# A graph-attention kernel: another head turned by VectorE in the first tile of each batch element, one head's copies moved to VectorE, and four small transposes moved between two others

## The chip, the cores and the metric

The kernel runs on one core of one Trainium2 chip. The metric is device time in microseconds (us) of one execution. Three executions of the kernel before took 3004.06, 3004.3 and 3010.76 us; their median is 3004.3 us.

## What is computed

The input is x with 16 batch elements of 1024 nodes and 256 features, and an integer adjacency matrix of 1024 x 1024 for each batch element. Two layers follow each other:

```python
# layer 0: masked attention, 8 heads of 32 features
h = relu(layernorm(x))
Q, K, V = h @ Wq.T + bq, h @ Wk.T + bk, h @ Wv.T + bv        # per head
scores = Q @ K.T * 32 ** -0.5;  scores[adj == 0] = -inf
x = x + (softmax(scores) @ V) @ Wo.T + bo
# layer 1: scores of the nodes with themselves, weighted by a vector for each kind of edge
h = relu(layernorm(x))
e_k = leaky_relu((h * a_k) @ h.T, 0.2)                       # symmetric
scores = e_k where adj == k + 1, else -9e15
x = x + softmax(scores) @ h
```

All data is fp32 (adj is int32). The inputs hold only the values 0 and 1 in adj, so layer 1 needs the first kind of edge alone; a second program for more kinds stands behind a branch and isn't run.

## The kernel before

**Tiles and steps.** A batch element is cut into 8 tiles of 128 rows (t = 0 to 7). The main loop has one step for each of the 128 tiles and one more. A step holds the work of several tiles at once, written out by hand in a loop over the heads h = 0 to 7: layer 0's attention of the present tile (`now`), the end of layer 0 of the tile before (`was`), layer 1 of a tile 9 steps back (`edge`) and 10 steps back (`edge_was`), and the projections of a tile 9 steps ahead (`piece`). The order on each engine is the order of this program; nothing reorders it. A step takes some 22 to 23 us, and mostly 25 to 27 us for t = 0.

**One head of layer 0.** TensorE makes the scores (L461, two matmuls into one half of PSUM's score space). VectorE adds the mask and takes the row's extreme in one instruction (L473, `softmax_max`). ScalarE takes the exponential (L490, `softmax_exp`, one turn of the loop later). Then the 128 x 1024 matrix must be turned, since the product with V needs the keys on the partitions. There are two ways:

- `turn`: 8 transposes of 128 x 128 on TensorE into two PSUM buffers of 128 x 512 (L590), each copied to SBUF into `pT` (L591). The copy is VectorE's for heads 0, 1, 4 and 5 (`MIXED`), ScalarE's for 2, 3, 6 and 7, unless the caller names an engine.
- `turn_blocks` and `place_blocks`: one VectorE instruction turns all blocks of 32 x 32 (L381), and 4 DMAs of 128 KB on SP's queue put the blocks where they belong in `pT` (L386).

`by_blocks(t)` tells which heads go the second way: 0, 1, 4 and 5 in tiles 1 to 6; 0, 1 and 4 in tile 7; 4 and 5 in tile 0. Heads in `MIXED` have their keys in another order, which suits the blocks. Where such a head is turned by TensorE after all, ScalarE's exponential writes with a permuted pattern into another buffer.

**Order around the change.** In turn h of a step: `scores(h)`; `softmax_max(h)`; `softmax_exp(h-1)`; head h-2 is turned. With t = 0, heads 5 and 6 of the tile before (`was`) are turned in turn h = 0, one after the other, head 5 with ScalarE's copies. Then `edge.score(0)` follows: the left half of layer 1's scores, for which a tile with t > 0 takes blocks that were kept from earlier tiles and transposes them (L627). In step t = 0 the edge tile has t = 7, so `score(0)` is 4 transposes. In turn h = 4 of a step with t = 0, `block` runs: it is `edge_was.gather(0)` (L698, 32 matmuls that read layer 1's turned matrix, placed by 4 DMAs that were issued in turn 0), then `was.combine(1)` (L526, 64 matmuls). The turn of head 2 is put off to turn h = 5 (`late_turn`), where heads 2 and 3 are turned one after the other, both with ScalarE's copies.

**SP's queue** issues, in program order: the keys of the next batch element (L360, 8 loads of 512 KB, spread over step t = 7 and the next step t = 0 by `KEY_STEPS`; the loads for heads 4 to 7 stand in turns 0, 2, 3 and 4 of step t = 0), the queries of the next tile (L428, turn 3), the block placements (L386), the stores of layer 0's result (L552) and of the output (L708). Each issue waits for the landing of the one 8 before it, because the queue's DMAs share 8 semaphores in turn. POOL's queue carries the other DMAs.

The lines that the text names: L461 scores, L473 softmax_max, L490 softmax_exp, L590/L591 turn_half, L381 blocks_of, L386 placed, L360 load_key, L428 load_queries, L526 combine, L698 gather, L627/L633 score, L656 edge.softmax_max, L541 output, L547 residual, L182/L183 layer norm statistics, L237/L249/L250 turn of the piece, L355 biased, L536 combined.

Of the kernel before, what the change touches and what calls it, by code (L numbers as in the profile page):

```python
# [24 lines left out]
NEG_INF = -9000000000000000.0  # L25
MASKED = -1e30
MIXED = (0, 1, 4, 5)
BY_BLOCKS = {7: (0, 1, 4), 0: (4, 5)}


def by_blocks(t):
    return BY_BLOCKS.get(t, MIXED)

# [14 lines left out]
def gnn_kernel(  # L48
# [18 lines left out]
    nc = tc.nc  # L67
# [719 lines left out]
    with tc.manual_schedule():  # L787
# [42 lines left out]
        piece, edge, edge_was = piece_next, None, None  # L830
# [8 lines left out]
        for s in range(B * NT + 1):  # L839
            b, t = divmod(s, NT)  # L840
# [7 lines left out]
            late_turn = None  # L848
# [14 lines left out]
            for h in range(HEADS):  # L863
# [49 lines left out]
                if h == 4 and not late_scores:  # L913
                    block()
                    late_turn = turning
                    load_keys(h, 1)
                    continue
                if h == 5 and late_turn:
                    late_turn.turn(2, 0)
                    late_turn.turn(2, 1)  # L920
                if h == 0 and t == 0 and was:
                    for half in range(2):
                        was.turn(HEADS - 3, half, nc.scalar.copy)
                if turning and th in by_blocks(turning.t):
                    turning.turn_blocks(th)
                    turning.place_blocks(th)
                elif turning and (h, t) != (HEADS - 1, NT - 1):
                    turning.turn(th, 0)
                    turning.turn(th, 1)
# [3 lines left out]


                if h == 0:
                    if edge:
                        edge.score(0)
                    if gone:
                        gone.normed()
                    if edge_was:  # L940
                        edge_was.turn_blocks()
                        edge_was.place_blocks()
# [57 lines left out]
            gone, was, now, nxt = was, now, nxt, nxt2  # L1000
            edge_was, edge = edge, edge_nxt
# [8 lines left out]
        for i in range(1, len(tiles) + 2):  # L1010
            edge = tiles[i] if i < len(tiles) else None
# [75 lines left out]
```

## Time and profile before

| | |
|---|---|
| runs | 3004.06, 3004.3, 3010.76 us |
| the profiled execution's own time | 3006.89 us |
| its span (first to last instruction) | 3005.0 us |
| TensorE clock granted | 0.998 |
| busy: TensorE, ScalarE, VectorE, GpSimd | 2903.3, 2635.5, 2495.4, 2171.0 us |
| DMA moved | 704.03 MB, mean 234 GB/s |

The profile is one execution. The page counts the busy time of each engine, groups the instructions by line and tile, and names for idle time what ended it. The timeline lists the instructions of a window in order of time; the windows view gives each engine's busy time and the share of time in which the 16 DMA engines were busy; the issue view gives the time from a DMA's issue to its landing. Times within a step are given below as us from the start of the span.

### The profile page before, as it was taken

To read this page: it belongs to the slowest core of one execution; us is meant where nothing else is said; L and a number is where in the kernel's file an instruction comes from. 1 tells how busy PE (TensorE), PEld (TensorE's weight loads), DVE (VectorE), ACT (ScalarE), POOL (GpSimd) and SP (SyncE) were. 2 spreads that over 40 slices of the span, in tenths; PEclk is the share of its full clock that TensorE was granted. 3 is DMA by queue.
4 is the path that set the end of the run, shared out by engine and by line. 5 is a ranking of instruction groups with operands and counts; after the bars stand their busy time and mean duration, and the time that the engine had idled before them with its cause. 6 is when DMAs were issued, how large, how long until landed. Compare 5 with 4: busy or idle time off the path is not lost. (4 is left out here: it accounts for less than half of the span.)

```text
span 3005.0 us, 95721 instructions
## 1 busy us (share of the span) xinstructions
PE 2903.3 (97%) x36594; PEld 2234.0 (74%) x36594; DVE 2495.4 (83%) x4405; ACT 2635.5 (88%) x5191; POOL 2171.0 (72%) x2999
## 2 busy tenths in 40 slices
PE   7889999999999999999999999999999999999998
PEld 5777777777777777777777777777777777777664
DVE  5888888888888888878888887888888888788875
ACT  5999989999898999999999998998989999898882
POOL 3767877777787777778778777777877777786542
PEclk9999999999999999999999999999999999999999
DMA  7787877778778887877878777787787878777763
GB/s 243 233 259 215 248 229 243 250 227 261 227 227 254 239 260 218 243 247 230 269 222 245 239 237 249 227 267 222 231 255 232 263 219 243 245 230 250 196 174 100
DMA packets 607041, 704.03 MB, mean 234 GB/s; under 512 B 64305, under 2 KB 537777, under 8 KB 606577
## 3 DMA queue, kind: packets, MB, share of 16 engines
q1 hardware_dynamic: 537504, 485.68, 54.4%
q0 software_dynamic: 66960, 210.04, 21.7%
q8 instruction: 294, 4.82, 0.7%
q10 hardware_dynamic: 2112, 2.10, 0.2%
q14 instruction: 171, 1.39, 0.1%
HBM read 252.98 MB, written 134.22 MB: 129 GB/s over the span
## 5 line engine op out<-in xcount | busy, mean ns | idle before, releaser
L473 DVE CUSTOM_DVE_ANT_0 p<-s,neg 128x1024 f32<-128x1024 f32 x1024 | 1238.6, 1210 | 344.8 <-PE s L461 324.6
L490 ACT ACTIVATE p<-p,nmx 128x1024 f32<-128x1024 f32 x1024 | 1236.4, 1214 | 51.6 <-DVE nmx L473 43.1
L461 PE MATMUL s<-k,qt 128*128 128x512 f32 x2048 | 743.2, 445 | 30.4 <-DMA k<-kd 8.3
L591 ACT COPY pT<-trp 128x512 f32<-128x512 f32 x1056 | 566.5, 593 | 77.5 <-PE trp L590 77.1
L590 PE MATMUL trp<-ident,p 128*128 128x128 f32 x4480 | 587.3, 274 | 27.4 <-ACT pT L591 15.0
L590 PEld LDWEIGHTS trp<-ident,p 128*128 128x128 f32 x4480 | 516.0, 140 | 118.9 <-ACT pT L591 30.2
L381 DVE STREAM_TRANSPOSE blocks<-p 128x1024 f32<-128x1024 f32 x472 | 585.2, 1240 | 11.1 <-ACT p L680 10.6
L526 PE MATMUL acc<-pT,v 128*32 128x128 f32 x16384 | 507.8, 273 | 9.3 <-ACT full L309 8.9
L526 PEld LDWEIGHTS acc<-pT,v 128*32 128x32 f32 x16384 | 453.4, 110 | 80.9 <-issue 36.1
L698 PE MATMUL acc<-h,pT 128*32 128x256 f32 x8192 | 510.0, 381 | 1.9 <-DMA pT<-blocks 1.6
L441 POOL TENSOR_SCALAR neg<-adj 128x1024 bf16<-128x1024 int32 x128 | 467.8, 3655 | 11.9 <-ACT neg L453 1.9
L676 POOL TENSOR_TENSOR sel<-sel,less 128x1024 f32<-128x1024 f32 x120 | 287.8, 2398 | 201.7 <-ACT less L665 201.7
L461 PEld LDWEIGHTS s<-k,qt 128*128 128x128 f32 x2048 | 312.4, 190 | 153.0 <-issue 82.5
L698 PEld LDWEIGHTS acc<-h,pT 128*32 128x32 f32 x8192 | 265.3, 110 | 190.7 <-issue 48.8
L633 PE MATMUL s<-h1T,ha 128*128 128x512 f32 (+2 forms) x744 | 272.8, 490 | 2.8 <-ACT h1T L569 2.8
L490 ACT ACTIVATION_READ_ACCUMULATOR p<-p,nmx 128x1 f32 x1024 | 213.3, 208 | 0.0
L330 POOL DMA_DIRECT2D kd<-halves x240 | 172.1, 766 | 35.5 <-POOL halves L314 35.4
L314 POOL TENSOR_TENSOR halves<-full,halves 128x256 fp32r<-128x256 f32 x240 | 176.5, 735 | 20.0
L674 POOL TENSOR_SCALAR less<-top 128x1 f32<-128x1 f32 x120 | 31.9, 266 | 213.0 <-DVE top L656 212.9
L647 ACT COPY mirror<-s 128x128 f32<-128x128 f32 (+3 forms) x208 | 76.1, 393 | 122.5 <-DVE top L656 102.9
L324 POOL DMA_DIRECT2D qd<-halves x240 | 177.8, 787 | 7.1
L633 PEld LDWEIGHTS s<-h1T,ha 128*128 128x128 f32 x744 | 126.7, 190 | 70.8 <-issue 44.8
(117 smaller groups left out, 4321.3 us busy)
## 6 DMA issues: line engine op xcount, KB each, us to landing
pT<-blocks SPq DMA_DIRECT2D x2368, 128.0 KB, 3.6
qt<-qd SPq DMA_DIRECT2D x128, 512.0 KB, 4.7
k<-kd SPq DMA_DIRECT2D x128, 512.0 KB, 6.8
adj<-in_adj POOLq DMA_DIRECT2D x127, 512.0 KB, 6.1
qd<-halves POOLq DMA_DIRECT2D x240, 256.0 KB, 4.0
kd<-halves POOLq DMA_DIRECT2D x240, 128.0 KB, 4.3
xb<-in_x POOLq DMA_DIRECT2D x128, 128.0 KB, 4.9
x1d<-x SPq DMA_DIRECT2D x128, 128.0 KB, 5.1
```

The costliest lines, as they stand in the source:

```text
L324: nc.gpsimd.dma_start(out=qds[self.b][self.first, oc].rearrange("p u w n -> p u (w n)"), in_=halves.unsqueeze(1).to_broadcast([P, 2, 2 * P]),)
L381: nc.vector.transpose(blocks.rearrange("p b j q -> p j b q"), p)
L441: nc.gpsimd.tensor_scalar(self.neg, self.adj, 0.0, MASKED, ALU.is_equal, ALU.mult)
L461: nc.tensor.matmul(self.ps[:, cols], lhsT=self.qt[:, h, :], rhs=keysets[self.b][h][:, cols], start=True, stop=True,)
L473: nc.vector.tensor_tensor_reduce(out=p, in0=sides[h in self.second], in1=self.neg, scale=-SCALE, scalar=FLOOR, op0=ALU.add, op1=ALU.min, a ...
L490: nc.scalar.activation(to, of, AF.Exp, bias=nmx, scale=-1.0, accum_out=self.sums[:, h : h + 1])
L526: nc.tensor.matmul(sums_place[r * HD : (r + 1) * HD, g * P : (g + 1) * P], lhsT=vs[self.b][:, j, place_of(h) : place_of(h) + HD], rhs=self ...
L590: nc.tensor.transpose(tr[:, j, :], p[:, jj * P : (jj + 1) * P], ident)
L591: copy(pT[:, half * 4 : half * 4 + 4, :], tr)
L633: nc.tensor.matmul(self.side[:, cols], lhsT=self.ha[:, c, :], rhs=h1T[:, c, cols], start=(c == 0), stop=(c == NC - 1),)
L676: nc.gpsimd.tensor_tensor(self.sel, self.sel, self.less, ALU.subtract)
L698: nc.tensor.matmul(self.sums[a * HD : (a + 1) * HD, :], lhsT=self.pT[:, j, a], rhs=h1s[self.b][:, j, :], start=(j == 0), stop=(j == NT - 1),)
```

## The change

Three edits, all in steps with t = 0 (one for each of the 16 batch elements, and the last step for the third edit):

1. Head 0 of tile 0 goes by blocks: VectorE's block transpose and 4 DMAs take the place of 8 TensorE transposes and 2 VectorE copies. Its exponential is then written in plain order, in place.
2. The two copies of head 2, turned late, go to VectorE instead of ScalarE.
3. `edge.score(0)` stands between the turns of heads 5 and 6 of the tile before instead of after both.

```diff
-BY_BLOCKS = {7: (0, 1, 4), 0: (4, 5)}
+BY_BLOCKS = {7: (0, 1, 4), 0: (0, 4, 5)}
...
                 if h == 5 and late_turn:
-                    late_turn.turn(2, 0)
-                    late_turn.turn(2, 1)
+                    late_turn.turn(2, 0, nc.vector.tensor_copy)
+                    late_turn.turn(2, 1, nc.vector.tensor_copy)
                 if h == 0 and t == 0 and was:
                     for half in range(2):
                         was.turn(HEADS - 3, half, nc.scalar.copy)
+                    if edge:
+                        edge.score(0)
...
                 if h == 0:
-                    if edge:
+                    if edge and (t or not was):
                         edge.score(0)
```

## The prediction

> **What bounds the kernel now.** I read the page's busy times first, then the timeline of one step with t = 0, then the DMAs of that step.
>
> ```profile
> PE 2903.3 (97%) x36594; PEld 2234.0 (74%) x36594; DVE 2495.4 (83%) x4405; ACT 2635.5 (88%) x5191; POOL 2171.0 (72%) x2999
> ```
>
> TensorE is busy 97% of the span, so eight transposes less should count in full: 16 steps of about 1 us. But that is an average. The change touches steps with t = 0 alone, so one of these must be read; I took the one from 1288.26 to 1313.97 us. TensorE's timeline there (start, duration, instruction, idle time before it):
>
> ```profile
> 1288.83 1.04 PE L590 MATMUL trp<-ident,p 128*128 128x128 f32 x8
> 1290.11 1.15 PE L590 MATMUL trp<-ident,p 128*128 128x128 f32 x8 [0.24 <-ACT pT L591]
> 1291.09 0.60 PE L627 MATMUL s<-ident,mirror 128*128 128x128 f32 x4
> 1291.44 0.72 PE L461 MATMUL s<-k,qt 128*128 128x512 f32 x2
> ...
> 1293.90 0.71 PE L461 MATMUL s<-k,qt 128*128 128x512 f32 x2
> 1294.92 1.15 PE L590 MATMUL trp<-ident,p 128*128 128x128 f32 x8 [0.30 <-ACT pT L591]
> 1295.90 0.49 PE L627 MATMUL s<-ident,mirror 128*128 128x128 f32 x3
> ...
> 1299.69 2.57 PE L698 MATMUL acc<-h,pT 128*32 128x256 f32 x31
> ...
> 1304.15 0.73 PE L461 MATMUL s<-k,qt 128*128 128x512 f32 x2
> ...
> 1306.11 1.04 PE L590 MATMUL trp<-ident,p 128*128 128x128 f32 x8
> 1307.46 1.14 PE L590 MATMUL trp<-ident,p 128*128 128x128 f32 x8 [0.32 <-ACT pT L591]
> 1308.36 0.71 PE L461 MATMUL s<-k,qt 128*128 128x512 f32 x2
> ```
>
> The three bracketed waits are what the edits aim at: 5/6 (edit 3), head 0 (edit 1), 2/3 (edit 2). The line between them matters more: the gather L698 takes 2.57 us here. Later in the same step 32 matmuls of L698 stand at 1.93 us (1310.36). It waits inside, for its matrix `pT`, which SP's DMAs place. SP's timeline and, for the fourth of these placements (issued 1294.64), the issue view:
>
> ```profile
> 1291.62 0.55 SPq L360 DMA_DIRECT2D k<-kd  x1
> 1292.28 3.96 SPq L386 DMA_DIRECT2D pT<-blocks  x4
> 1296.28 1.30 SPq L360 DMA_DIRECT2D k<-kd  x2
> ...
> ```
>
> ```profile
> DMA to landing us min/median/max: 5.9/5.9/5.9
> ```
>
> So the last of the four pieces lands at 1300.52, 12.26 us into the step, and the scores of head 5 start at 1304.15, which is 3.63 us later: just 32 matmuls of L698 (pitch 1.75, from 1310.36 to 1312.11) and 64 of L526 (1.86, from 1312.11 to 1313.97). I took the same two times in the other steps with t = 0. In batch elements 4, 9 and 14 the fourth piece lands 13.87, 11.56 and 13.41 us into the step, head 5's scores start at 17.50, 15.20 and 17.04, and the steps take 27.31, 25.00 and 26.86 us. The first difference is 3.63 to 3.64 in all 14 steps that have a gather, and 9.8 us follow it in 13 of them. The steps differ only in when that DMA lands. The windows view says why it is late:
>
> ```profile
> 1288.26:1304.15 15.89, 15.35 (x180) 13.00 (x177) 11.05 (x19) 14.75 (x27) 10.10 (x18) 1.00 1.03 373
> ```
>
> The last two columns: the DMA engines are busy all the time (1.03) at 373 GB/s. Four loads of keys and one of queries, 512 KB each, crowd here. **In a step with t = 0 the DMA queue, not TensorE, sets when the second half starts.**
>
> **The change part by part.** *Edit 1* removes 8 transposes and their wait: from the scores at 1293.90 to L627 at 1295.90 are 2.00 us, and scores alone have a pitch of 0.56 (1308.36 to 1308.91 shows 0.55), so TensorE gains 1.44 us. VectorE gives up two copies (1.28 as a pair at 1295.80) for one block transpose (1.24, L381): level. ScalarE writes head 0's exponential in order: 2.16 us at 1292.28 against 1.16 for an unpermuted one, 1.0 us less. SP gets 4 issues of 128 KB. *Edit 3*: head 6's transposes wait for the PSUM buffer that ScalarE copies until about 1290.05; the four of L627 (pitch 0.35) now fill this time, and head 6 starts no later than now, so TensorE gains 0.35.
>
> Both lie before the gather, 1.79 us together, and neither moves its matrix: that comes from VectorE's transpose of `sel`, which needs only the step's first scores, and its DMAs stand on SP behind the key loads, ahead of the new issues. TensorE would reach head 3's scores at 1295.9, before their keys land: that load was issued at 1289.86 and landed at 1296.56. Head 4's keys land at 1298.64, and the gather's last piece at 1300.52. So the gain turns into waits at L461 and L698. **I cost edits 1 and 3 at nothing.** Cover gone, they are worth up to 1.79 us a step; 1.2 if head 4's scores wait for VectorE's L656, which head 0's block transpose and L656 itself (1.24 + 1.19) put at about 1297.8 against scores at 1299.05 now.
>
> The new DMAs: their first can go out when VectorE's transpose ends: head 2's `softmax_max` starts 0.35 earlier than now and ends at 1295.5, 1.24 more make 1296.7. Each issue then waits for the landing of the eighth before it. They go out from 1296.7 to 1299.3, and the loads of head 6's and 7's keys follow instead of going out at 1296.94 and 1298.66. 512 KB at 369 GB/s (the DMA rate of this stretch) are 1.42 us of DMA time; SP's four issues are 2.4 to 2.6 us. Head 7's keys, which landed at 1306.34 (7.68 after the issue), would land between 1307.8 and 1308.9; they are read at 1309.72. That is covered, and so are head 6's, which land earlier and are read at 1308.36. The queries loaded between them are for the next step.
>
> *Edit 2* lies behind the gather, where nothing hides it. ScalarE's pair of copies takes 1.08 us and starts 0.71 after the transposes (1306.82 against 1306.11). VectorE is free at 1306.23, so its pair starts as soon as the first half is there, 0.64 after (what an idle ScalarE shows elsewhere: transposes at 1404.52, copy at 1405.16), and takes 1.28. Its second copy ends 1.92 after the transposes' start instead of 1.79; the second half of head 3's transposes waits for it. **That is 0.13 us a step lost.** Bounds: a gain of 0.32 if the whole wait went, a loss of 0.35 if all of the pair's 0.20 and another 0.15 of a late start counted. I take 0.13, since the rows are direct. On VectorE the copies push residual and norms (1306.37 to 1308.00) behind 1308.03, and head 6's `softmax_max` from 1309.11 to about 1309.7. Next in line would be the next step's first scores, which need head 7's: these end at 1312.61 and the scores start at 1313.97, so 1.36 us cover 0.6. ScalarE's 1.08 us less release nobody: its next copies wait for TensorE (0.26 idle at 1308.16).
>
> *Other steps.* In the first step of all (41.1 to 67.7) there is no gather; ScalarE is late there and head 3's transposes wait 0.96 us, while VectorE is free: 0.8 us gained. In the step at 198.8 (no gather either) head 7's `softmax_max` ends only 0.22 us before the next scores: the copies cost about 0.4.
>
> Sum: 14 x 0.13 - 0.8 + 0.4 = +1.4 us on the profiled execution's 3006.89 us (span 3005.0), so 3008.3. That execution is 2.6 us above the median of 3004.3; on the median I forecast 3005.7, say 3006.
>
> *The skill on two points.* The Trainium skill, "DMA: Bandwidth & Descriptors", section "Queues, rings and completion order", says that an engine takes a ring's descriptors in order but that completion isn't first in, first out. In this trace the pieces land before the keys that were issued after them (1300.52 against 1301.81), so the rows speak for order; by the page's warning the sum would be that of the second rival below. "VectorE: DVE Perf Modes", section "Rules for kernel authors", would leave a full 128 x 128 turn to TensorE. By that rule edit 1 is to be left out, and the sum would lose its part, which the rows put at nothing anyway.
>
> **The rivals.** *The gate gives way.* If the placements landed earlier, or the waits inside L698 were small, the gains would reach the step's end: 1.2 to 1.79 us in 14 steps, less 1.4 above, 15 to 24 us: 2980 to 2989 (I take 2986). For it speaks the 97%; against it the constant 3.63 us in 14 of 14 steps.
>
> *The new DMAs push the gate.* They go out from 1296.7 on, while the gather's pieces are still under way (until 1300.52). If the 16 DMA engines shared their time among all that is under way, these pieces would land up to 1.42 us later; past zero it decides at once, since the gather has no slack. Price: 14 x 1.42 + 1.4 = 21 us: 3026. Against it: the next keys, 512 KB, went out at 1296.28 already, and still landed after.
>
> *Edit 2 gains instead.* The 2/3 wait of 0.32 goes: 14 x 0.32 + 0.8 = 5 us less: 2999, still within the bound. That the change does something else than it says I exclude: the program's instruction order holds the three moves as told and no others.
>
> **How the numbers follow.** Forecast 0.70; edit 2 gains 0.12; the gate gives way 0.10; the DMAs push it 0.08. About 0.3% (9 us) is what a measurement of this kernel can tell from no change. Faster 0.10, same 0.82, slower 0.08. The range takes in the forecast, edit 2's bounds (14 x -0.32 and +0.35: 2999 to 3009), the runs' own spread (6.7 us above the median) and a part of both outer rivals: 2992 to 3016.
>
> **What would show it.** Right: in steps with t = 0 the start of head 5's scores still follows the fourth placement's landing by 3.63 us and that landing stays 11.6 to 13.9 us into the step; TensorE's waits move from L590 to L461 and L698, named DMA; head 3's transposes still wait about 0.3 us, now for VectorE. Wrong: steps with t = 0 shorter by over a microsecond, the landing at another time, or waits for keys at heads 6 and 7.

## The result, and the profile after

| | kernel before | changed kernel |
|---|---|---|
| median of 20 runs (lowest, highest), us | 3010.15 (3003.87 to 3012.76) | 3014.53 (3006.91 to 3019.45) |
| the profiled execution's own time; span, us | 3006.89; 3005.0 | 3012.56; 3010.7 |

The ratio is 1.0017 [1.0009, 1.0024]: some 5 us slower, which by the prediction's bound of 0.3% is "the same". The forecast of 3006 is 8.5 us too low. Of that, 5.9 us are the base: the three runs shown had a median of 3004.3, and 20 runs have one of 3010.15. The rest is the change: the medians differ by 4.4 us, and the forecast gave it 1.7 (1.4 before rounding).

The busy times on the changed kernel's page:

```profile
PE 2888.7 (96%) x36466; PEld 2218.8 (74%) x36466; DVE 2517.8 (84%) x4421; ACT 2602.5 (86%) x5159; POOL 2167.4 (72%) x2999
```

TensorE is busy for 14.6 us less than before (2903.3), and the span is longer. To see why, read a step with t = 0 again. This is TensorE's timeline of the changed kernel in the same batch element as in the prediction; the step begins at 1291.91:

```profile
1292.48 1.03 PE L590 MATMUL trp<-ident,p 128*128 128x128 f32 x8
1293.35 0.60 PE L627 MATMUL s<-ident,mirror 128*128 128x128 f32 x4
1293.79 1.11 PE L590 MATMUL trp<-ident,p 128*128 128x128 f32 x8
1294.65 0.71 PE L461 MATMUL s<-k,qt 128*128 128x512 f32 x2
1297.16 0.71 PE L461 MATMUL s<-k,qt 128*128 128x512 f32 x2
1297.70 0.49 PE L627 MATMUL s<-ident,mirror 128*128 128x128 f32 x3
...
1301.48 0.70 PE L461 MATMUL s<-k,qt 128*128 128x512 f32 x2 [1.73 <-DVE top L656]
1303.49 0.69 PE L461 MATMUL s<-k,qt 128*128 128x512 f32 x2 [0.43 <-DMA k<-kd]
1304.17 2.59 PE L698 MATMUL acc<-h,pT 128*32 128x256 f32 x31
...
1308.65 0.73 PE L461 MATMUL s<-k,qt 128*128 128x512 f32 x2
...
1311.99 1.25 PE L590 MATMUL trp<-ident,p 128*128 128x128 f32 x8 [0.35 <-DVE pT L591]
```

L627 now stands between the two turns, and their wait of 0.24 us is gone; head 0's transposes and their 0.30 us are gone too. The time comes back as waits of 1.73 and 0.43 us at the scores of heads 3 and 4. (The 1.73 is put down to VectorE's L656, but that stands behind head 3's scores in the program and can't have held them; head 3's keys landed at 1301.35, just before the scores.) The late turn still waits, 0.35 us, now for VectorE. SP's timeline of the same step shows the four new issues at 1301.42, ahead of the keys of heads 6 and 7:

```profile
1295.42 3.84 SPq L386 DMA_DIRECT2D pT<-blocks  x4
1299.30 0.84 SPq L360 DMA_DIRECT2D k<-kd  x1
1301.42 3.17 SPq L386 DMA_DIRECT2D pT<-blocks  x4
1304.64 0.62 SPq L360 DMA_DIRECT2D k<-kd  x1
1305.37 0.54 SPq L428 DMA_DIRECT2D qt<-qd  x1
1305.95 0.59 SPq L360 DMA_DIRECT2D k<-kd  x1
```

The gather's fourth piece was issued at 1297.96, and its issue view answers:

```profile
DMA to landing us min/median/max: 7.1/7.1/7.1
```

It lands at 1305.02, and head 5's scores start 3.63 us later, as before.

I took the same times in all steps with t = 0 of batch elements 2 to 15, in each kernel. "Landing" is that of the fourth piece; "rest" runs from head 5's scores to the step's end. All are means in us, the two landings and head 7's scores from the step's begin:

| kernel | length | landing | head 5's scores after it | rest | head 7's keys land | head 7's scores |
|---|---|---|---|---|---|---|
| before | 25.93 | 12.58 | 3.63 | 9.71 | 18.24 | 21.69 |
| changed | 26.46 | 12.80 | 3.69 | 9.96 | 21.19 | 22.20 |

### The profile page after: what moved, and what is told of

Its sections match the earlier page's. It is cut to its first block, busy times and chain, and to the rows that moved or that the text cites. A ratio compares the mean times of both kernels' runs of the same rounds, so it can differ in the third digit from the quotient of the medians.

```text
span 3010.7 us, 95592 instructions
## 1 busy us (share of the span) xinstructions
PE 2888.7 (96%) x36466; PEld 2218.8 (74%) x36466; DVE 2517.8 (84%) x4421; ACT 2602.5 (86%) x5159; POOL 2167.4 (72%) x2999
## 3 DMA queue, kind: packets, MB, share of 16 engines
q0 software_dynamic: 66960, 210.04, 21.6%
## 5 line engine op out<-in xcount | busy, mean ns | idle before, releaser
L490 ACT ACTIVATE p<-p,nmx 128x1024 f32<-128x1024 f32 x1024 | 1218.3, 1196 | 53.3 <-DVE nmx L473 51.1
L461 PE MATMUL s<-k,qt 128*128 128x512 f32 x2048 | 743.7, 445 | 56.0 <-DMA k<-kd 28.4
L591 ACT COPY pT<-trp 128x512 f32<-128x512 f32 x1024 | 549.9, 592 | 99.9 <-PE trp L590 99.6
L381 DVE STREAM_TRANSPOSE blocks<-p 128x1024 f32<-128x1024 f32 x488 | 605.0, 1240 | 12.3 <-ACT p L680 10.6
L590 PE MATMUL trp<-ident,p 128*128 128x128 f32 x4352 | 571.5, 274 | 20.4 <-ACT p L490 13.0
L590 PEld LDWEIGHTS trp<-ident,p 128*128 128x128 f32 x4352 | 502.6, 141 | 105.0 <-ACT p L490 26.5
L698 PE MATMUL acc<-h,pT 128*32 128x256 f32 x8192 | 508.4, 381 | 2.1 <-DMA pT<-blocks 2.0
L461 PEld LDWEIGHTS s<-k,qt 128*128 128x128 f32 x2048 | 312.0, 190 | 182.7 <-issue 91.1
L698 PEld LDWEIGHTS acc<-h,pT 128*32 128x32 f32 x8192 | 263.3, 110 | 191.9 <-issue 50.3
```

The lines of the kernel that those rows point to most:

```text
L381: nc.vector.transpose(blocks.rearrange("p b j q -> p j b q"), p)
L461: nc.tensor.matmul(self.ps[:, cols], lhsT=self.qt[:, h, :], rhs=keysets[self.b][h][:, cols], start=True, stop=True,)
L490: nc.scalar.activation(to, of, AF.Exp, bias=nmx, scale=-1.0, accum_out=self.sums[:, h : h + 1])
L590: nc.tensor.transpose(tr[:, j, :], p[:, jj * P : (jj + 1) * P], ident)
L591: copy(pT[:, half * 4 : half * 4 + 4, :], tr)
L698: nc.tensor.matmul(self.sums[a * HD : (a + 1) * HD, :], lhsT=self.pT[:, j, a], rhs=h1s[self.b][:, j, :], start=(j == 0), stop=(j == NT - 1),)
```

## The experiments

The theory of the prediction: the landing of the gather's pieces gates a step with t = 0, so what TensorE gains ahead of it is waited away. Rivals: the gate gives way; the four new DMAs delay the gather's pieces; and, formed on seeing the 21.19 above, the new DMAs cost time because they hold up what stands behind them on SP's queue, the keys of heads 6 and 7.

All runs in one table; the edits are told below it. Ratios are to the kernel before, on the same chip. The clock is the mean of TensorE's granted clock over that kernel's executions (before: 0.9972, 0.9974 and 0.9977 in the three sets). The last column lists TensorE's waits of 1.5 us and more ahead of scores (L461) between 370 and 2800 us of the profile; an asterisk marks those during or after which the granted clock fell to 0.50, which is the subject of a later part.

| kernel | median, us | ratio | clock | waits, us |
|---|---|---|---|---|
| changed | 3014.53 | 1.0017 [1.0009, 1.0024] | 0.9958 | 1.52 2.77 1.73 3.44* 2.33 2.30 |
| e1_head0 | 3014.93 | 1.0019 [1.0009, 1.0028] | 0.9955 | 1.53 1.84* 1.50 2.25* |
| e2_copies | 3012.07 | 1.0004 [0.9994, 1.0013] | 0.9980 | 2.04* |
| e3_score | 3009.45 | 0.9995 [0.9986, 1.0004] | 0.9975 | none (before: none) |
| e13_no_copies | 3011.82 | 1.0002 [0.9993, 1.0011] | 0.9960 | 1.96 1.51 1.68 2.91* 2.38* 2.75* |
| e1_late | 3010.08 | 1.0002 [0.9993, 1.0012] | 0.9963 | 1.76 2.09* 2.26* |
| gm0_gather_late | 2999.97 | 0.9970 [0.9961, 0.9979] | 0.9976 | 1.59 |
| gm3_gather_late | 3001.89 | 0.9979 [0.9970, 0.9987] | 0.9975 | none |
| gm13_gather_late | 3026.32 | 1.0053 [1.0038, 1.0067] | 0.9943 | 11 waits, 1.50 to 3.85*, three with * |
| nk0_no_key_loads | 2990.10 | 0.9937 [0.9925, 0.9950] | 0.9975 | none |
| nk13_no_key_loads | 2975.90 | 0.9891 [0.9877, 0.9906] | 0.9977 | none |
| gm13_late_place | 3007.38 | 0.9996 [0.9985, 1.0006] | 0.9952 | 2.92* 2.13 2.02* 2.62* |
| gm13_turn2_early | 2992.85 | 0.9948 [0.9936, 0.9960] | 0.9970 | 2.56* 1.83 1.80 1.56 1.69 2.90* |

### Each edit alone, and edits 1 and 3

Edit 1 alone changes the one line of `BY_BLOCKS`; edit 2 alone the two calls with `nc.vector.tensor_copy`; edit 3 alone the place of `edge.score(0)`; the fourth kernel has edits 1 and 3.

> Edit 1 alone (head 0 of tile 0 by blocks, nothing else). Theory A (the gather's landing sets the step, the gain before it is waited away, the new DMAs come too late to matter): 0 us, between -1 and +1. Rival B (the four new DMAs take DMA time from the gather's pieces and from the keys of head 7): +2 to +4 us, that is the greater part of the +5 us (ratio 1.0017) of the whole change; in its profile the keys of head 7 land 20.5 to 22.5 us into a step with t = 0 (17.4 to 19.6 before) and one or two steps wait for them. Rival C (TensorE's time counts): -15 us or more.

> Edit 2 alone (head 2's late copies by VectorE). Theory A: the part of a step with t = 0 behind the scores of head 5 grows from 9.80 to 9.96 us, 14 x 0.15 = 2 us slower, the whole of it; nothing ahead of these scores changes. Rival D (edit 2 is the whole of the +5 us, because later work on VectorE is late as well): +4 to +5 us.

> Edit 3 alone (the four transposes of layer 1's left scores between the turns of heads 5 and 6). Theory A: 0 us, between -1 and +1; the wait of 0.24 us ahead of head 6's transposes goes and comes back at the keys or at the gather. Rival C: 15 x 0.35 = 5 us faster.

> Edits 1 and 3 without edit 2. Theory A: 0 us, between -1 and +1, the part behind head 5's scores back at 9.80 us. Rival B: +2 to +4 us, as edit 1 alone. Rival C: 14 x 1.2 to 1.8, that is 17 to 25 us faster.

Only edit 1 differs from no change by more than its interval; its 0.19%, 5.7 us, lies above what Theory A (-1 to +1) and Rival B (+2 to +4) expected. In the profiles the gate is untouched: the landing is at 12.73, 12.80, 12.85 and 12.89 us, and with the four new DMAs (first and last) it is no later than without them. Edit 2 shows as 9.96 us of rest instead of 9.80 in most steps. The parts add up to +0.18% (0.19 + 0.04 - 0.05), the whole has +0.17%. Edits 1 and 3 together, +0.02%, are below the sum of their own, +0.14%; the intervals, 0.09 to either side, let this stand open. So edit 1 alone shows a loss, and edits 1 and 3 together, which hold edit 1, show none.

### Edit 1 with its placements behind the key loads

```diff
                     turning.turn_blocks(th)
-                    turning.place_blocks(th)
+                    if (turning.t, th) != (0, 0):
+                        turning.place_blocks(th)
...
                     load_keys(h, 1)
+                    if now and not t:
+                        now.place_blocks(0)
```

> Edit 1 alone, but its four placement DMAs are issued behind the last key load of the step (turn 4) instead of in turn 2. The profiles so far have the gather's fourth piece at 12.58 to 12.85 us without and at 12.73 to 12.89 with the new DMAs, so they do not push the gate. Rival B2 (edit 1's +5.7 us come from the keys of heads 6 and 7 and the queries, which now stand behind the new DMAs): the keys of head 7 land at 18 us again and the time is 0 to +1.5 us. Theory E (the cost is the 512 KB of DMA as such, or VectorE's block transpose, wherever the DMAs stand): +4 to +6 us as before.

The same transposes, the same four DMAs, issued after head 7's keys: +0.02% instead of +0.19%, and these keys land at 18.84 us instead of 20.83. Theory E's +4 to +6 us lie outside the interval, which ends at +0.12%, 3.6 us. It speaks for the place in the queue as a part of edit 1's cost. It isn't the whole proof: the intervals of the two ratios touch (1.0009 to 1.0012), and the profile of e1_head0 shows a wait for head 7's keys in one step only, of 0.2 us.

### The gate moved out of the way

The first half of the gather is taken from `block` and put next to the second half in turn 7 (gm0); with edit 3 (gm3); with edits 1 and 3 (gm13):

```diff
-                if edge_was and not t:
-                    edge_was.gather(0)
                 if was:
                     was.combine(1)
...
                     if edge_was:
+                        if not t:
+                            edge_was.gather(0)
                         edge_was.gather(1)
```

> The kernel before, with one change of order: in steps with t = 0 the first half of the gather is made in turn 7, next to the second half, instead of ahead of the combine in turn 4. Theory A: the gather's DMA is then off the path. TensorE goes from head 4's scores straight to the combine; head 5's scores then wait for their keys (landed 13.5 to 15.1 us) or for the combine, some 13.3 to 14.5 us into the step, and the step gets 0.3 to 1 us shorter: 4 to 14 us faster. If the gather's DMA were not the gate: 0 us.

> The same order with edit 3 alone. Theory A: as gm0_gather_late within 1.5 us, since the keys of heads 3 to 5 gate the scores ahead of it and not the 0.35 us of edit 3. Rival C2: 5 us faster than gm0_gather_late.

> The same order with edits 1 and 3. Theory A with B2: with the gather out of the way the next gates are the keys, and edit 1's DMAs delay those of heads 6 and 7 to 20 to 22 us, while the scores of head 7 would be due at about 19.5: slower than gm0_gather_late by 1 to 2 us a step, 14 to 28 us. Rival C2 (without the gate TensorE's time counts): faster than gm0_gather_late by up to 14 x 1.2, that is 17 us.

Without the gate the kernel before is 10 us faster, so the gate is a bound of these steps. Edit 3 adds nothing to it. Edits 1 and 3 make it 26 us slower than gm0, because the next wait in line is head 7's keys. TensorE's timelines, first gm0, then gm13, each in batch element 3:

```profile
576.92 1.05 PE L267 MATMUL acc<-hT,wkT 128*128 128x128 f32 x8
577.73 0.71 PE L461 MATMUL s<-k,qt 128*128 128x512 f32 x2
```

```profile
591.27 1.05 PE L267 MATMUL acc<-hT,wkT 128*128 128x128 f32 x8
592.82 0.73 PE L461 MATMUL s<-k,qt 128*128 128x512 f32 x2 [0.50 <-DMA k<-kd]
```

In gm13 head 7's scores start 0.04 to 0.05 us after their keys land in 13 of 14 steps (means 21.31 and 21.26 us; in gm0 the keys land at 18.44 us and the scores start at 19.83, 1.48 us earlier, which is 20.7 us in 14 steps). In the changed kernel the gate hides most of this: the scores stand at 22.20.

### The key loads taken away

For batch elements 1 to 15, batch element 0's keys are used: 15 x 8 loads are left out. nk0 has no other edit, nk13 has edits 1 and 3.

```diff
     def load_key(b, h):
+        if b:
+            keysets.setdefault(b, {})[h] = keysets[0][h]
+            return
```

> The kernel before, without the key loads from batch element 1 on: the keys of element 0 are used for all (the computation leaves out 15 x 8 loads of 512 KB and uses wrong keys; everything else is done). Theory A: the DMA queue is then free around t = 0, the gather's pieces land before TensorE asks for them, and the steps with t = 0 are TensorE's own, 25.4 us each, as the best ones with the late gather: 7 to 14 us faster than the kernel before.

> Edits 1 and 3 on top of that, again without the key loads. Theory A: with the DMA queue free the 1.79 us that TensorE saves ahead of the gather reach the end of the step, less what VectorE holds back (its instruction of layer 1 ahead of head 4's scores): 1.2 to 1.8 us a step, 17 to 25 us faster than nk0_no_key_loads. If the gain were lost elsewhere than at the keys and the gather: 0 to 5 us.

nk0 is 19.0 us faster than the kernel before by the medians (3009.11 in this set), more than the 7 to 14 expected. The gather's piece lands at 9.51 us instead of 12.58, and the steps no longer follow it: they take 24.83 to 24.87 us in 13 of 14, while the piece lands anywhere from 8.94 to 10.58 us. Here edits 1 and 3 are worth what their transposes cost: steps of 24.76 and 23.79 us, 0.97 us x 14 = 13.6 us, and 14.2 us by the medians (2990.10 less 2975.90), less than the 17 to 25 expected. TensorE's timeline of nk13, a step with t = 0 (its L464 and L701 are L461 and L698):

```profile
1284.66 0.38 PE L519 MATMUL acc<-ident,wide 128*128 128x128 f32 x2
1284.80 0.71 PE L464 MATMUL s<-k,qt 128*128 128x512 f32 x2
...
1287.67 1.93 PE L701 MATMUL acc<-h,pT 128*32 128x256 f32 x32 [0.17 <-ACT full L309]
```

Head 3's scores follow at once, and the gather takes 1.93 us, not 2.59. So the edits do save TensorE's time; with the key loads in place it is waited away.

### Both causes answered, and head 2's turn moved

gm13_late_place is gm13 with the late placements of e1_late. gm13_turn2_early also turns head 2 in turn 4, behind `block`, with ScalarE's copies, in place of `late_turn` in turn 5.

> Late gather, edits 1 and 3, and head 0's placements behind the last key load. Theory A with B2: head 7's keys land at 18 to 19 us again and no longer hold its scores, so the 27 us that gm13_gather_late lost against gm0_gather_late come back; head 5's scores still wait for their keys (13.5 us and more), so only part of TensorE's gain shows: 0 to 7 us faster than gm0_gather_late (ratio 0.997 there), ratio 0.995 to 0.997. If the cost of edit 1 lay in VectorE or in the DMA bytes as such: above 1.

> As gm13_late_place, and head 2 is turned in turn 4 behind the combine, while TensorE waits for head 5's keys, instead of in turn 5. Theory A: the wait for these keys is filled with transposes (0.9 us) and the 2/3 wait (0.3 us) goes: up to 1.2 us a step, 5 to 15 us faster than gm13_late_place, ratio 0.990 to 0.995.

In the first one head 7's keys land at 18.52 us and its scores start at 19.84, as in gm0 (18.44 and 19.83); the same edits with the placements ahead of the keys had a ratio of 1.0053, and this one has 0.9996. So the place in the queue was the greater part of what held gm13_gather_late back. Still the run missed: I expected it at least as fast as gm0, and it is 7.4 us slower. One of its steps takes 29.83 us where the mean is 25.81. The windows view there: TensorE's idle time ahead of head 3's scores, 0.5 us of work, the stretch after it, and the next one (the third number from the right is the granted clock):

```profile
566.20:569.00 2.80, 0.00 (x0) 0.00 (x0) 1.61 (x3) 2.80 (x8) 0.66 (x1) 1.00 1.05 373
569.50:570.00 0.50, 0.50 (x6) 0.41 (x5) 0.09 (x1) 0.50 (x2) 0.46 (x2) 1.00 0.99 395
571.00:576.50 5.50, 5.09 (x67) 3.87 (x68) 2.71 (x7) 1.42 (x3) 5.34 (x5) 0.50 0.98 312
577.50:580.00 2.50, 1.89 (x14) 1.50 (x13) 2.40 (x7) 2.40 (x6) 2.44 (x6) 1.00 0.57 215
```

After 2.92 us of waiting for head 3's keys the clock is halved. In this profile that happens in three of the 14 steps, and their head 5's scores come 1.0, 1.2 and 2.3 us later after the landing than in most other steps (1.35 to 1.41). That is 4.5 us, the gain that these steps lack: in the two profiles they have the same mean length, 25.81 us. It isn't the 7.4 us themselves: the profiled executions differ by 3.7 us, and these lie in the first steps, the steps with t = 1 to 7 and the end.

gm13_turn2_early beats both kernels: 2992.85 us, 0.9948 [0.9936, 0.9960], 14.5 us below gm13_late_place. Its granted clock is higher as well (0.9970 against 0.9952), so not all of the 14.5 us need be the move itself.

### A cause that no theory had named: the clock is halved at some long waits

The same fall of the clock is in the changed kernel. In batch element 9, TensorE's timeline:

```profile
1664.98 0.38 PE L516 MATMUL acc<-ident,wide 128*128 128x128 f32 x2
1668.80 0.92 PE L461 MATMUL s<-k,qt 128*128 128x512 f32 x2 [3.44 <-DMA k<-kd]
1669.52 1.91 PE L590 MATMUL trp<-ident,p 128*128 128x128 f32 x8
```

and the windows view around it:

```profile
1665.30:1668.80 3.50, 0.06 (x2) 0.03 (x1) 1.72 (x3) 3.50 (x9) 1.18 (x3) 1.00 1.02 362
1669.50:1672.50 3.00, 3.00 (x15) 2.24 (x17) 2.62 (x5) 2.23 (x5) 2.92 (x4) 0.50 0.91 326
1673.00:1676.00 3.00, 3.00 (x89) 2.31 (x81) 0.55 (x2) 0.00 (x0) 2.92 (x2) 1.00 0.94 321
```

Eight transposes take 1.91 us there instead of 1.04 to 1.11, and head 5's scores come 4.47 us after the landing instead of 3.63. It is the one of 14 steps in which the 3.63 does not hold. Edits 1 and 3 gain time ahead of head 3's keys; the gain becomes one long idle stretch where the kernel before had transposes to do; and after some of these stretches the matmuls that follow run at half the clock.

The table of the experiments bears this out. The kernels with edit 1 and key loads have a mean clock of 0.9943 to 0.9970 and 3 to 11 long waits each; all others have 0.9972 to 0.9980 and none or one. nk13, which has edit 1 but no key loads to wait for, has 0.9977 and none. So it takes both.

The single runs point the same way. Of the changed kernel's 20 runs, the eight with a granted clock of 0.997 or 0.998 have a median of 3011.3 us, 1.2 us above the kernel before; the twelve with 0.993 to 0.996 have 3016.4, 6.2 us above it. In e1_head0's 11 runs time and clock go together as well (correlation -0.89). This is no proof, since a run with longer waits has both a longer time and a lower clock. No kernel here holds the clock up by itself, so what it costs in time is an estimate: 0.9958 against 0.9972 to 0.9977 is 0.0014 to 0.0019 x 3010 = 4.2 to 5.7 us of full-speed time, of which a part lies ahead of the landing and is waited away anyway. In the one profile 0.84 us (4.47 less 3.63) reached the step's end. And e1_late has a low clock (0.9963) without a longer time, so a lower mean clock doesn't always make the kernel slower.

## Why the prediction was right, and where it was off

**The gate: right.** With the edits, too, head 5's scores follow the fourth landing by 3.63 to 3.64 us in 13 of 14 steps, and the waits moved from L590 to L461. Removing the gather from there (gm0) and making the landing early (nk0) both sped the kernel up. The rival "the gate gives way" is refuted for this kernel: TensorE saved 14.6 us of busy time and none of it reached the end.

**The new DMAs push the gate: refuted at its price of 1.42 us a step.** The landing is at 12.80 us with them, and at 12.80 and 12.85 in e2_copies and e3_score without. The 12.58 of the kernel before lies within the differences from one execution to another (gm3_gather_late: 12.53).

**Edit 2: right.** Predicted 0.13 us a step; the rest went from 9.80 to 9.96, 0.15 to 0.16 us, 2 us over 14 steps. (By its runs alone, +0.04% [-0.06, +0.13], edit 2 can't be told from no change; the profiles show it.)

**Edits 1 and 3 at nothing: right as a gain, open as a loss.** As a gain it is nothing, as forecast. Measured together and without edit 2 (e13_no_copies), they cost +0.02% [-0.07, +0.11], which is the forecast's nothing within its interval. But edit 1 alone measured +0.19%, 5.7 us, and the whole change costs some 3 us more than was forecast, which edit 2 doesn't explain. Two steps of the working behind this term failed.

The first is the price of the new DMAs for the loads behind them. I wrote that head 7's keys "would land between 1307.8 and 1308.9", 19.5 to 20.6 us into the step, and called them covered. They land at 21.19 on average, at up to 22.39, and in batch elements 4 and 15 head 7's scores start 0.04 us after them; the rest of these two steps is 10.76 and 9.13 us instead of 9.96 and some 8.7 (e2_copies). The prediction had named waits for these keys as a sign of being wrong. The loads are not slower: from issue to landing they take 7.22 us, 7.26 before. They are issued 2.99 us later, at 13.97 us into the step instead of 10.98, where 1.42 to 2.6 us were charged. The new DMAs go out from 9.26 us on, on average, not from 8.4.

The second: a wait was counted as free once it stood ahead of the gate, where a long wait can cost clock behind it.

**First steps: not to be told from one execution.** The first step of all is 4.9 us shorter (21.6 us instead of 26.5), not 0.8, but by the step at 198.8 all is given back: that step starts at 199.3. In other profiles the first step takes 26.6 us with edits 1 and 3 (e13_no_copies) and 24.3 with edit 2 alone, so its length isn't the edits' doing alone. At 376 us the changed kernel is 0.4 us late where the forecast had it 0.4 us early.

**Small readings.** In the stretch before the gate five loads of keys are issued, not four: head 3's, at 1289.86, is one of them. And the slowest of the three runs lies 6.5 us above their median, not 6.7. Neither changes the forecast.

The account of the two profiled executions, whose spans differ by 5.7 us: up to 376 us +0.4; the 14 steps with t = 0 +7.4; the steps with t = 1 to 7 between them +0.2; the end -2.3, for which I have no cause (in both kernels the clock falls there only after TensorE's last matmul). Of the 7.4, edit 2 is 2.1, waits for head 7's keys in two steps 1.2, the lost clock 0.8; these are 4.1 us. The other 3.1 to 3.3 are the later landing (0.22 x 14), which I take for chance, by the landings above. That the 4.1 comes near the 4.4 by the medians proves little, since single executions scatter: in the same 14 steps the profile of e2_copies has 7.0 us more than that of the kernel before, and that of e3_score 4.5, though their runs have ratios of 1.0004 and 0.9995.

The forecast is near the measurement in part by luck: its mechanism held, but a loss of some 3 us that it didn't have is small beside its range.

**Open:** how the loss divides between keys and clock; why edits 1 and 3 together don't show it; why the profiles of e1_head0, e13_no_copies and e1_late, but not that of the changed kernel, show 2 to 4 us more in the steps with t = 1 to 7.

## What to carry to other kernels

When a stage waits for a transfer, work removed from the waiting engine ahead of it buys nothing, however busy the engine is on average; look for the landing that the next stage follows at a constant distance. When work goes from an engine to a DMA queue, list what is issued behind the new transfers and when it is read. And a wait that grows is not neutral: in this kernel it could cost clock after it had ended, so read the granted clock behind each long wait.

## What the runs showed of the hardware

- The half clock lasts 3.41 us (1669.11 to 1672.52 in the changed kernel; as long in gm13_gather_late at 1328.01 and e13_no_copies at 2038.39), or twice that, 6.83 us, as in gm13_late_place at 570.40. At the waits with an asterisk it begins between 1.8 us before and 1.3 us after the matmuls have resumed. It came with waits of 1.84 us and more, but not with each: 2.77 us in the changed kernel at 936.39 left the clock at 1.00, while 1.92 us in gm13_gather_late did not.
- What decided in these runs was how the wait lay to a fixed grid in time. Within each profile the moments at which the clock fell are whole multiples of 3.413 us apart, to 0.005 us. Between 100 and 2900 us the 14 profiles have 11,483 windows of that grid. The clock fell at the end of 25 of them, in which TensorE was busy for 0.31 to 1.57 us. Every window with less than 1.48 us of busy time is among them, and none with more than 1.57. The changed kernel's wait of 3.44 us lay almost whole in one window, which ended at 1669.11. The 2.77 us were cut by a window's end at 935.24, with 1.80 and 2.12 us of busy time on the two sides (first number after the length):

```profile
1665.70:1669.11 3.41, 0.31 (x2) 0.30 (x3) 1.32 (x3) 3.41 (x9) 1.06 (x4) 1.00 1.06 357
931.83:935.24 3.41, 1.80 (x17) 1.56 (x15) 3.41 (x5) 3.41 (x6) 0.92 (x2) 1.00 1.05 407
935.24:938.65 3.41, 2.12 (x12) 1.53 (x12) 1.46 (x5) 3.41 (x10) 1.88 (x3) 1.00 1.03 384
```

- The Trainium skill, "TensorE: Matmul & The Clock Gate", section "What's actually happening", describes a free-running window of about 3.4 us and a clock that is halved after at least one idle window. The length of 3.41 us and the grid agree with that. That a whole window has to be idle is not what these runs show: windows in which TensorE was busy for up to 1.57 us were enough.
- In this kernel requests issued later did not delay those under way: four more DMAs of 128 KB behind the gather's pieces left their landing where it was (12.73 to 12.89 us with them, 12.80 and 12.85 without). The loads behind them were issued later, by 2.99 us for head 7's keys, and took as long as before from issue to landing (7.22 us, 7.26 before).
